# Masked attention with residual on one core: the last batch's outputs, gathers and partial outputs are placed elsewhere, and its short chunk is computed in four blocks

## The chip, the cores and the metric

The kernel runs on one core of a Trainium2 chip. The core has five engines that follow programs of their own and meet through semaphores: PE (matmul, with its weight loads PEld), DVE (VectorE), ACT (ScalarE), POOL (GpSimd) and SP (SyncE). SP does no arithmetic here; it issues DMAs. POOL and ACT issue some too. Sixteen DMA engines carry all of them. The metric is the time of one execution on the device in microseconds; the time before is the median of three runs, 651.81 us (649.6 to 653.38).

## The reference

`x` is 8 x 512 x 1024 (batch, features, tokens), the mask `cond_2048` is 8 x 1024 of zeros and ones, and `Wq`, `Wo` are 512 x 512. All of it is float32.

```python
xt = jnp.transpose(x, (0, 2, 1))
q = xt @ Wq.T                                    # queries, keys and values alike
qh = q.reshape(B, T, NH, dk).transpose(0, 2, 1, 3)       # 8 heads of 64
scores = scale * jnp.einsum('bhqd,bhkd->bhqk', qh, qh)
logits = (scores * cmask + (1.0 - cmask) * NEG) * rmask  # mask on keys, and on queries
attn = jax.nn.softmax(logits, axis=-1)
ctx = jnp.einsum('bhqk,bhkd->bhqd', attn, qh)
out = ctx.transpose(0, 2, 1, 3).reshape(B, T, D) @ Wo.T
return x + jnp.transpose(out, (0, 2, 1))
```

About half of the tokens are masked. A masked token is no key, and as a query all of its logits are zero, so its context is the plain mean of all values.

## The kernel before

The kernel computes attention for the kept tokens of a batch only, at most 543 of them (`NK` = 544), with the mean of all tokens as the last column. The 544 tokens are four chunks of 128 and a short one of 32 (`LAST` = 4, `END` = 32). Two other versions of the program, for masks that keep more tokens, stand behind a branch and do not run.

A batch has four pairs of heads. `pairs` lists all 32 pairs (batch, pair), and the main loop of `late` runs over them; each has five slots, k = 0 to 4, one for each chunk of keys, the short one first. A slot issues `scores` for its chunk (matmuls, then the exponentials on ACT), some fixed steps, and the steps that `slots_of` put into it. The order in the source is the order on each engine: nothing is reordered afterwards, and an engine that waits holds up all that stands behind it. The words (7,1) mean pair 1 of batch 7, the last batch.

The steps that matter here:

- `end_attend`, `go_on_attend`, `attend`, `attend_last`: products of the exponentials with the values (line 730 and 748). `inverses` (824 to 832) makes the reciprocal sums `ris` on DVE. For most pairs `invert` sends them through DRAM (`row<-rt`, `rb<-row`, on SP) to spread them over the partitions; for the last two pairs PE does it in `spread` (810). `contexts` (859 to 868) multiplies the context by them on DVE and gives `cT`. `contexts` of a pair comes two pairs later, at k = 0; for (7,2) it came one pair later, at k = 1 of (7,3).
- `output(b, i)`: chunk i of a batch's output, four matmuls (883), a copy on ACT (892) and a store to `od` in DRAM by POOL (894). For the short chunk `output` already computes four blocks of 128 columns side by side in the four column groups of PE. Batch 6's outputs stand in (7,1) and (7,2).
- `load_rows(b, i)` (941, SP): block i, of eight, of the original tokens from `xd`, into `g`. `fetch(b, i)` (977, POOL): a gather from `od` by the tokens' places, which adds to `g`; a `keep_step` (974) before it ties it to its slot. It waits for all stores of `od`. `finish_blocks(b, i)` (947, DVE): turns `g` into `xr`; after the eighth, SP issues four writes of 512 KB to `out` (954). There is one `xr` buffer. The dictionaries `ROWS_LAST`, `FETCH_LAST` and `FINISH_LAST` say in which slots of batch 7 batch 6's blocks take these steps.
- The last batch ends otherwise: `begin_output` (903, copy 911) makes the product of the first three pairs of each chunk in (7,3), and after `attend_last` `end_output` adds the fourth (919 on PE, 927 on DVE) and stores with SP (933). Then `fetch_last` gathers (963, POOL), `finish_tokens` turns on PE (992), adds on DVE (993) and writes from ACT's queue (994).

`woT` holds its columns in another order, (a, d, f) instead of (d, a, f), which is why `end_output` adds through rearranged views.

Of the kernel before, what the change touches and what calls it, by code (L numbers as in the profile page):

```python
# [13 lines left out]
ALU = mybir.AluOpType  # L14
# [292 lines left out]
def attention_of_kept_tokens(ctx, tc, x, mask, wq, wo, out, ident, wqT, woT, verdict, flag):  # L307


    nc = tc.nc  # L310
    B, D, T = x.shape
    P = 128
    DK = D // NH
    SCALE = 1.0 / math.sqrt(DK)
    ND = D // P
# [4 lines left out]
    A = P // Q  # L320
    NQ = 4
    NC = -(-LONG // P)
    LAST = NC - 1
# [4 lines left out]
    sizes, places = [], []  # L328
# [48 lines left out]
    xs, xbars, xmeans, xds, xins, xcs, parts, searches = {}, {}, {}, {}, {}, {}, {}, {}  # L377
# [292 lines left out]
    es, rbs, cTs, shares = {}, {}, {}, {}  # L670
# [132 lines left out]
    def spread(pair, inv):  # L803

        rb = rbs[pair] = sb.tile([P, W], F32, tag="rb", name="rb_%d_%d" % pair)
        for at, n in ((0, LAST), (LAST, 1)):
            pt = bank("rb_%d_%d" % (pair[1], at))
            for i in range(n):
                for h in range(2):
                    nc.tensor.matmul(  # L810
                        pt[h * DK : (h + 1) * DK, i * P : (i + 1) * P],
                        inv[:, h, at + i : at + i + 1].to_broadcast([P, DK]),
                        ident,
                        start=True,
                        stop=True,
                    )
            nc.scalar.copy(rb[:, at * P : (at + n) * P], pt[:, : n * P])
# [46 lines left out]
    def contexts(pair):  # L864
        sum_last(pair)
        cT, rb = cTs[pair], rbs.pop(pair)
        nc.vector.tensor_tensor(cT, cT, rb[:, :NK], ALU.mult)
        nc.vector.tensor_copy(cT[:, NK - 1 : NK], qTs.pop(pair)[:, W - 1 : W])


    ods, gs, xrs = {}, {}, {}
# [23 lines left out]

    partials = {}

    def begin_output(b, i):

        n = sizes[i]  # L900
        po = bank(f"pa_{b}_{i}")
        for pr in range(ND - 1):
            nc.tensor.matmul(
                po[:n, :],
                cTs[b, pr][:, i * P : i * P + n],
                woT[:, pr, :],
                start=(pr == 0),
                stop=(pr == ND - 2),
            )
        pa = sb.tile([P, D], F32, tag="xin", name=f"pa_{b}_{i}", bufs=NC)  # L910
        nc.scalar.copy(pa[:n, :], po[:n, :])
        partials[i] = pa

    def end_output(b, i):
        n = sizes[i]
        if i == 0:
            ods[b] = dr.tile([NK, D], F32, tag="od", name=f"od_{b}")
        po = bank(f"po_{b}_{i}")
        nc.tensor.matmul(
            po[:n, :],  # L920
            cTs[b, ND - 1][:, i * P : i * P + n],
            woT[:, ND - 1, :],
            start=True,
            stop=True,
        )
        oc = sb.tile([P, D], F32, tag="oc", name=f"oc_{b}_{i}", bufs=NC)
        nc.vector.tensor_tensor(
            oc[:n, :].rearrange("p (d a f) -> p a d f", d=ND, a=A),
            po[:n, :].rearrange("p (a d f) -> p a d f", d=ND, a=A),
            partials[i][:n, :].rearrange("p (a d f) -> p a d f", d=ND, a=A),  # L930
            ALU.add,
        )
        nc.sync.dma_start(ods[b][places[i], :], oc[:n, :])

    def in_blocks(t):
        return t.rearrange("(k f) (a n) -> a f k n", f=Q, a=A)
# [67 lines left out]
    pairs = [(b, pr) for b in range(B) for pr in range(ND)]  # L1004

    def slots_of(p):

        b, pr = pairs[p]
        todo = [[] for _ in range(NC)]
        before = pairs[p - 1] if 0 < p < len(pairs) - 1 else None  # L1010
        behind = pairs[p + 1] if p + 1 < len(pairs) else None
        ahead = pairs[p + 2] if p + 2 < len(pairs) else None

        def do(k, f, *args):
            todo[k].append(lambda: f(*args))

        late = p == 2
        new = pr == 2 and b + 1 < B
        by_vector = nc.vector.tensor_copy

        def project_with_values():
            project(ahead, 0, lambda end: turn_values(behind, end))
            copy_values(behind)

        def mean_with_values():
            pt = bank(f"mean_{b + 1}")
            turn_values(behind, pt[:, KH : KH + P])
            put_mean(b + 1, pt, lambda: copy_values(behind))

        def project_with_top(hf, tag="t"):  # L1030
            project(ahead, hf, lambda to: turn_top(behind, to), tag)
            bias_of(behind)

        if before:
            do(0, go_on_attend, before)
        due = []
        if pr == 1 and b + 1 == B:
            due = [0, 1]
        elif pr > 0 and 0 < b < B - 1:
            due = {1: (0, 1, LAST), 2: (2,), 3: (3,)}[pr]  # L1040
        if not new:
            for i in due:
                do(3, output, b - 1, i)
        if p == 0:
            do(0, project, behind, 1)
            do(1, values, behind)
            do(1, lengths_of, behind)
            do(1, project, ahead, 0)
            do(2, project, ahead, 1)
            do(3, bias_of, behind)  # L1050
        elif late:
            do(1, values, behind)
            do(2, lengths_of, behind)
            do(2, end_attend, before)
            do(2, put_mean, b + 1)
            do(2, collect, b + 1, 0)
            do(3, bias_of, behind)
            do(3, collect, b + 1, 1, by_vector, "a")
            do(3, collect, b + 1, 2, None, "a")
            do(4, collect, b + 1, 3)  # L1060
            do(4, collect, b + 1, 4)
            for hf in range(2):
                do(4, project, ahead, hf, None, "a")
        elif new:
            do(1, mean_with_values)
            do(2, end_attend, before)
            do(3, collect, b + 1, 0, by_vector)
            do(3, collect, b + 1, 1, by_vector)
            do(3, collect, b + 1, 2, by_vector, "a")
            do(3, collect, b + 1, 3, None, "a")  # L1070
            do(3, collect, b + 1, 4, by_vector)
            do(3, lengths_of, behind)
            for i in due:
                do(3, output, b - 1, i)
            do(3, project_with_top, 0)
            do(3, project, ahead, 1, None, "a")
        elif ahead:
            do(1, project_with_values)
            do(2, lengths_of, behind)
            do(2, end_attend, before)  # L1080
            do(3, project_with_top, 1)
        elif behind:
            do(1, output, b - 1, LAST - 1)
            do(1, values, behind)
            do(2, lengths_of, behind)
            do(2, end_attend, before)
            do(3, bias_of, behind)
            do(3, output, b - 1, LAST)
        if p == ND - 1:
            for d in range(ND):  # L1090
                do(3 + d // 2, turn_weights, woT, "wo", d, None, "at"[d // 2], True)
        if pr == 1 and b + 1 == B:
            do(4, output, b - 1, 2)
        if p + 1 == len(pairs):
            for i in range(NC):
                do((1, 1, 2, 3, 4)[i], begin_output, b, i)
        return todo

    def load_weights(w, nm, queue=None):
# [163 lines left out]
    def late(n):  # L1263
# [36 lines left out]
            (1, 1): (6, 7),  # L1300
        }
        FINISH = {(0, 4): (0, 1), (1, 1): (2, 3), (1, 2): (4, 5), (1, 4): (6, 7)}
        FETCH_LAST = {(2, 4): (0, 1, 2), (3, 0): (3, 4, 5), (3, 1): (6, 7)}
        FINISH_LAST = {(3, 1): (0, 1, 2), (3, 2): (3, 4, 5), (3, 3): (6, 7)}
        ROWS = {(2, 2): (0, 1), (2, 3): (2, 3), (3, 0): (4, 5), (3, 2): (6, 7)}
        ROWS_LAST = {(2, 0): (0, 1, 2), (2, 1): (3, 4, 5), (2, 2): (6, 7)}
        for p, pair in enumerate(pairs):
            b, pr = pair
            before = pairs[p - 1] if p else None
            todo = slots_of(p)  # L1310
            for k, c in enumerate(order):
# [5 lines left out]
                if k == 0 and before:  # L1317
                    if p + 1 < len(pairs):
                        invert(before)
                    else:  # L1320
                        inv = inverses(before)
                if p + 1 == len(pairs):
                    if k == 1:
                        spread(before, inv)
                        contexts(before)
                if b > 1:
                    for i in FETCH.get((pr, k), ()):
                        keep_step(pair, c)
# [1 line left out]
                if b + 1 == B:  # L1330
                    for i in FETCH_LAST.get((pr, k), ()):
                        keep_step(pair, c)
# [31 lines left out]
                if b > 0:  # L1364
                    for i in (ROWS if b + 1 < B else ROWS_LAST).get((pr, k), ()):
                        load_rows(b - 1, i)
# [7 lines left out]
                if b + 1 == B:  # L1374
                    for i in FINISH_LAST.get((pr, k), ()):
                        finish_blocks(b - 1, i)
# [134 lines left out]
```

## Time and profile before

| what | us |
|---|---|
| median of three runs | 651.81 |
| the profiled execution | 656.09 |
| its span | 654.4 |
| PE busy in the span | 614.3 |
| ACT, DVE, POOL busy | 378.3, 359.8, 211.1 |
| from the last products on PE (625.64) to the first gather of batch 7 (632.96) | 7.3 |
| from that gather to the end of the span | 21.4 |

A row of the timeline reads: start, length, engine, line, operation, what is written and read, how many instructions are merged in it, and in brackets how long the engine had been idle and what ended that. SPq and ACTq are DMA issues; their length is the issue, not the transfer. A row of a stretch reads: stretch, its length, busy time of PE, PEld, DVE, ACT and POOL with instruction counts, PE's granted clock, the busy share of the DMA engines and GB/s. In the DMA view q1 is SP's queue, q0 POOL's and q10 ACT's; a line of 40 digits is the busy share of the DMA engines in tenths over the window cut in 40.

### The profile page before, as it was taken

Reading aid. Unit: us, or ns where it says so; the run is one execution under the profiler, and the core shown is the slowest. Engines: PE = TensorE matmul, PEld = TensorE weight load, DVE = VectorE, ACT = ScalarE, POOL = GpSimd, SP = SyncE. Lnnn points to the kernel's source line nnn. Section 1 sums busy time; section 2 is a strip of 40 time slices with the busy share of each in tenths; the row PEclk is TensorE's granted clock in tenths of the full one; section 3 lists DMA queues with packets and bytes.
Section 4 is the critical chain, followed back from the end, with each engine's and each line's share of the span. In section 5 each row is a group of like instructions: output and inputs, shape, how many; then the busy total and the mean of one; then the engine's idle time right before and its main releaser. Section 6 shows DMA issues by size and latency. Waiting matters only on the chain. (4 is left out here: it accounts for less than half of the span.)

```text
span 654.4 us, 15913 instructions
## 1 busy us (share of the span) xinstructions
PE 614.3 (94%) x6078; PEld 380.5 (58%) x6078; DVE 359.8 (55%) x1034; ACT 378.3 (58%) x1004; POOL 211.1 (32%) x313
## 2 busy tenths in 40 slices
PE   4789799999999999999999999999999999998964
PEld 3756466656665666566665666566665666554323
DVE  6449556335465566746465558566575425444543
ACT  4266558754766577754776577664775556554400
POOL 5620400140067004830176004720275006305422
PEclk7799899999999999999999999999999999999985
DMA  7666612454588757977598756975795635566677
GB/s 237 187 199 166 233 57 67 141 168 133 147 178 214 244 172 186 180 246 230 172 182 257 228 173 155 199 244 187 196 179 164 198 102 94 111 162 188 112 220 219
DMA packets 94543, 116.62 MB, mean 178 GB/s; under 512 B 11911, under 2 KB 61639, under 8 KB 94462
## 3 DMA queue, kind: packets, MB, share of 16 engines
q1 hardware_dynamic: 74030, 75.20, 38.6%
q0 software_dynamic: 16208, 38.25, 25.2%
q10 hardware_dynamic: 4224, 2.10, 1.1%
q8 instruction: 49, 0.80, 0.5%
q14 instruction: 32, 0.26, 0.1%
HBM read 72.81 MB, written 42.70 MB: 177 GB/s over the span
## 5 line engine op out<-in xcount | busy, mean ns | idle before, releaser
L692 ACT ACTIVATE e<-s,bias 128x544 f32<-128x544 f32 x256 | 180.5, 710 | 75.6 <-PE s L684 58.9
L684 PE MATMUL s<-qT 64*64 64x272 f32 x2048 | 154.8, 398 | 6.5 <-ACT e L692 4.9
L748 PE MATMUL av<-e,v 64*64 64x272 f32 x1920 | 132.4, 392 | 0.0
L598 PE MATMUL pq<-xc,wqT 128*128 128x272 f32 x512 | 131.4, 401 | 0.0
L598 PEld LDWEIGHTS pq<-xc,wqT 128*128 128x128 f32 x512 | 93.3, 190 | 36.8 <-issue 21.0
L684 PEld LDWEIGHTS s<-qT 64*64 64x64 f32 x2048 | 77.2, 133 | 55.8 <-ACT e L692 13.4
L883 PE MATMUL po<-woT,cT 128*128 128x512 f32 (+1 forms) x448 | 108.9, 439 | 0.0
L894 POOL DMA_DIRECT2D od<-oc x56 | 30.2, 544 | 238.5 <-ACT oc L892 237.7
L977 POOL DMA_INDIRECT g<-od,block_origin x56 | 90.1, 1610 | 30.9 <-DVE ends L721 8.1
L748 PEld LDWEIGHTS av<-e,v 64*64 64x64 f32 x1920 | 76.6, 134 | 38.1 <-issue 2.1
L664 DVE TENSOR_REDUCE m<-pq 128x1 f32<-128x128 f32 x28 | 8.2, 292 | 132.0 <-ACT qT L610 107.5
L883 PEld LDWEIGHTS po<-woT,cT 128*128 128x128 f32 (+1 forms) x448 | 46.5, 149 | 54.6 <-issue 53.2
L608 ACT COPY qT<-pq 128x272 f32<-128x272 f32 x64 | 24.6, 385 | 69.7 <-PE pq L655 29.0
L947 DVE STREAM_TRANSPOSE xr<-g 128x512 f32<-128x512 f32 x56 | 57.9, 1099 | 7.6 <-DMA g<-od,block_origin 7.5
L645 DVE TENSOR_REDUCE len<-sq 128x10 f32<-128x640 f32 x32 | 25.8, 805 | 60.4 <-ACT sq L643 60.3
L974 POOL COPY step<-e 1x1 f32<-1x1 f32 x75 | 23.7, 316 | 90.7 <-ACT e L692 90.5
L692 ACT ACTIVATION_READ_ACCUMULATOR e<-s,bias 128x1 f32 x256 | 50.5, 197 | 0.0
L544 POOL DMA_INDIRECT xin<-xd,source x40 | 38.7, 968 | 16.6 <-issue 5.6
L892 ACT COPY oc<-po 128x512 f32<-128x512 f32 (+1 forms) x35 | 18.0, 515 | 44.0 <-PE po L883 43.5
L474 DVE STREAM_TRANSPOSE xt<-x 128x1024 f32<-128x1024 f32 x28 | 34.7, 1241 | 1.5 <-DMA xd<-xt 0.9
L532 DVE TENSOR_SCALAR_CACHE_REDUCE junk<-rank,key 128x1024 f32<-128x1024 f32 (+4 forms) x35 | 34.9, 998 | 0.0
L721 DVE CUSTOM_DVE_ANT_0 junk<-el,part 128x272 f32<-128x272 f32 x64 | 27.3, 427 | 6.6 <-ACT el L709 4.4
(175 smaller groups left out, 674.0 us busy)
## 6 DMA issues: line engine op xcount, KB each, us to landing
xd<-xt SPq DMA_DIRECT2D x120, 128.0 KB
x<-in_x_dram SPq DMA_DIRECT2D x56, 256.0 KB
g<-xd SPq DMA_DIRECT2D x56, 256.0 KB
out_dram<-xr SPq DMA_DIRECT2D x28, 512.0 KB
rb<-row SPq DMA_DIRECT2D x60, 160.0 KB
od<-oc POOLq DMA_DIRECT2D x28, 256.0 KB
rank<-ranks SPq DMA_DIRECT2D x6, 512.0 KB
x<-in_x_dram POOLq DMA_DIRECT2D x8, 256.0 KB
```

What stands on the lines that cost most here:

```text
L474: nc.vector.transpose(xt.rearrange("p k (d f) -> p k d f", d=ND), xs[b][r][:, :, at : at + n].rearrange("p d (k t) -> p k d t", t=Q),)
L532: nc.vector.tensor_scalar(junk[:, :n], rank[:, i * P :], key[:, col], 0.0, ALU.is_le, ALU.add, accum_out=found[:, col])
L544: nc.gpsimd.indirect_dma_start(out=xin[:n, :], out_offset=None, in_=xds[b], in_offset=bass.IndirectOffsetOnAxis(ap=searches[b][2][:n, i : ...
L598: nc.tensor.matmul(pq[:, :KH], wqT[:, d, pr * P : (pr + 1) * P], xcs[b][:, d, cols], start=(d == 0), stop=(d == ND - 1),)
L684: nc.tensor.matmul(ss[h][r * DK : (r + 1) * DK, hf, :KH], qT[heads[h], c * P + r * DK : c * P + (r + 1) * DK], qT[heads[h], queries[hf]], ...
L692: nc.scalar.activation(e[:, :, h, :], ss[h][:, :, :KH], AF.Exp, bias=bias, scale=SCALE, accum_out=sums[pair[1] % 2][:, h, c : c + 1],)
L721: nc.vector.tensor_tensor_reduce(junk[:, :KH], e[:, 0, h, :], parts[b], 1.0, 0.0, ALU.mult, ALU.add, ends[pr % 2][:, h : h + 1])
L748: nc.tensor.matmul(avs[pair][hf][head, :KH], v[keys, c, head], e[keys, hf, h, :], start=(c == 0 and not crossed), stop=(c == LAST - 1 and ...
L883: nc.tensor.matmul(po[k * n : (k + 1) * n, :w], cTs[b, pr][:, i * P : i * P + n], woT[:, pr, k * w : (k + 1) * w], start=(pr == 0), stop=( ...
L894: nc.gpsimd.dma_start(ods[b][places[i], k * w : (k + 1) * w], oc[k * n : (k + 1) * n, :w])
L947: nc.vector.transpose(xr.rearrange("p (d a) (t i) -> p a d t i", a=A, i=NT)[..., i], gs[b, i].rearrange("p (a d f) -> p a d f", a=A, f=Q),)
L977: nc.gpsimd.indirect_dma_start(out=gs[b, i], out_offset=None, in_=ods[b], in_offset=bass.IndirectOffsetOnAxis(ap=block_origin[:, b, i : i ...
```

## The change

Four things are changed, all for batches 6 and 7, and nothing else.

1. Batch 6's outputs all stand in (7,1): chunk 0 in slot 2, 1 and 2 in slot 3, 3 and the short one in slot 4. Before, (7,1) had 0 and 1 in slot 3 and 2 in slot 4, and (7,2) had 3 in slot 1 and the short one in slot 3.
2. Batch 6's blocks: loads in (7,1) slots 2 to 4 and (7,2) slot 0, gathers in (7,2), turning from (7,2) slot 3 to (7,3) slot 2. Before, loads in (7,2), gathers from (7,2) slot 4 to (7,3) slot 1, turning in (7,3) slots 1 to 3.
3. In (7,3) `spread` and `contexts` of (7,2) stand in slot 0 and not in slot 1, and the partial outputs in slots 1, 2, 3, 4, 4 and not in 1, 1, 2, 3, 4.
4. The short chunk of batch 7 is computed in four blocks of 128 columns side by side, in `begin_output` as in `end_output`, each with a strided view of `woT`; its addition runs over 128 x 128 and not 32 x 512, and it is stored with four DMAs, two from SP's queue and two from ACT's.

```diff
+    def add_product(b, i, pr, po, start, stop):
+        n = sizes[i]
+        parts = P // n
+        w = D // parts
+        tokens = cTs[b, pr][:, i * P : i * P + n]
+        if parts == 1:
+            nc.tensor.matmul(po, tokens, woT[:, pr, :], start=start, stop=stop)
+            return
+        in_order = woT[:, pr, :].rearrange("p (a d f) -> p d a f", a=A, d=ND)
+        for k in range(parts):
+            nc.tensor.matmul(
+                po[k * n : (k + 1) * n, :w],
+                tokens,
+                in_order[:, k * ND // parts : (k + 1) * ND // parts, :, :],
+                start=start,
+                stop=stop,
+            )
...
         for pr in range(ND - 1):
-            nc.tensor.matmul(po[:n, :], cTs[b, pr][:, i * P : i * P + n], woT[:, pr, :], ...
+            add_product(b, i, pr, po, pr == 0, pr == ND - 2)
-        nc.scalar.copy(pa[:n, :], po[:n, :])
+        nc.scalar.copy(pa[:, :w], po[:, :w])
...
-        nc.sync.dma_start(ods[b][places[i], :], oc[:n, :])
+        else:
+            nc.vector.tensor_tensor(oc[:, :w], po[:, :w], partials[i][:, :w], ALU.add)
+        for k in range(parts):
+            queue = nc.scalar if k % 2 else nc.sync
+            queue.dma_start(ods[b][places[i], k * w : (k + 1) * w], oc[k * n : (k + 1) * n, :w])
...
         if pr == 1 and b + 1 == B:
-            due = [0, 1]
+            due = [1, 2]
+            do(2, output, b - 1, 0)
...
-            do(1, output, b - 1, LAST - 1)
             do(1, values, behind)
...
-            do(3, output, b - 1, LAST)
...
         if pr == 1 and b + 1 == B:
-            do(4, output, b - 1, 2)
+            do(4, output, b - 1, LAST - 1)
+            do(4, output, b - 1, LAST)
         if p + 1 == len(pairs):
             for i in range(NC):
-                do((1, 1, 2, 3, 4)[i], begin_output, b, i)
+                do((1, 2, 3, 4, 4)[i], begin_output, b, i)
...
-        FETCH_LAST = {(2, 4): (0, 1, 2), (3, 0): (3, 4, 5), (3, 1): (6, 7)}
-        FINISH_LAST = {(3, 1): (0, 1, 2), (3, 2): (3, 4, 5), (3, 3): (6, 7)}
+        FETCH_LAST = {(2, 0): (0,), (2, 1): (1, 2), (2, 2): (3, 4), (2, 3): (5, 6), (2, 4): (7,)}
+        FINISH_LAST = {(2, 3): (0,), (2, 4): (1, 2), (3, 1): (3, 4, 5), (3, 2): (6, 7)}
-        ROWS_LAST = {(2, 0): (0, 1, 2), (2, 1): (3, 4, 5), (2, 2): (6, 7)}
+        ROWS_LAST = {(1, 2): (0, 1), (1, 3): (2, 3), (1, 4): (4, 5), (2, 0): (6, 7)}
...
-                if p + 1 == len(pairs):
-                    if k == 1:
-                        spread(before, inv)
-                        contexts(before)
+                if p + 1 == len(pairs) and k == 0:
+                    spread(before, inv)
+                    contexts(before)
```

More of the change, by code (lines that the diff above doesn't have):

```diff
@@ L896, in attention_of_kept_tokens @@
     partials = {}
+    def add_product(b, i, pr, po, start, stop):
[15 more added lines that the diff above has]
+            )
     def begin_output(b, i):
-        n = sizes[i]
         po = bank(f"pa_{b}_{i}")
         for pr in range(ND - 1):
[L903 to L909, printed above, removed]
+            add_product(b, i, pr, po, pr == 0, pr == ND - 2)
+        w = D // (P // sizes[i])
         pa = sb.tile([P, D], F32, tag="xin", name=f"pa_{b}_{i}", bufs=NC)
-        nc.scalar.copy(pa[:n, :], po[:n, :])
+        nc.scalar.copy(pa[:, :w], po[:, :w])
         partials[i] = pa
@@ L915, in end_output @@
         n = sizes[i]
+        parts = P // n
+        w = D // parts
         if i == 0:
@@ L918, in end_output @@
         po = bank(f"po_{b}_{i}")
[L919 to L925, printed above, removed]
-        oc = sb.tile([P, D], F32, tag="oc", name=f"oc_{b}_{i}", bufs=NC)
[L927 to L933, printed above, removed]
+        add_product(b, i, ND - 1, po, True, True)
+        oc = sb.tile([P, D], F32, tag="oc", name=f"oc_{b}_{i}", bufs=NC)
+        if parts == 1:
+            nc.vector.tensor_tensor(
+                oc.rearrange("p (d a f) -> p a d f", d=ND, a=A),
+                po.rearrange("p (a d f) -> p a d f", d=ND, a=A),
+                partials[i].rearrange("p (a d f) -> p a d f", d=ND, a=A),
+                ALU.add,
+            )
+        else:
[3 more added lines that the diff above has]
+            queue.dma_start(ods[b][places[i], k * w : (k + 1) * w], oc[k * n : (k + 1) * n, :w])
     def in_blocks(t):
```

## The prediction

> **What bounds the kernel now.** I read, in this order: the page's busy times, the busy times by stretch of the last batch, the chain of waits, the timeline of the last 100 us engine by engine, and the DMA view in windows where a transfer is late.
>
> ```profile
> span 654.4 us, 15913 instructions
> PE 614.3 (94%) x6078; PEld 380.5 (58%) x6078; DVE 359.8 (55%) x1034; ACT 378.3 (58%) x1004; POOL 211.1 (32%) x313
> ```
> ```profile
> 552.40:576.40 24.00, 24.00 (x195) 13.42 (x198) 14.79 (x38) 11.94 (x31) 8.31 (x11) 1.00 0.51 104
> 576.40:595.50 19.10, 18.32 (x214) 10.13 (x206) 6.54 (x27) 9.98 (x26) 3.23 (x7) 1.00 0.77 221
> 595.50:617.80 22.30, 20.54 (x128) 8.44 (x126) 10.64 (x17) 10.24 (x25) 13.31 (x15) 1.00 0.69 123
> ```
> ```profile
> 640.55 5.73 DMA g<-od,origin
> ```
> The three stretches are the pairs (7,1), (7,2) and (7,3); the first two columns are the length and PE's busy time. PE sets the pace, so moving matmuls is free unless PE comes to wait. After PE's last attention, the chain is stores, gathers and writes; its longest piece is one gather of 5.73 us. So the change is worth the PE waits that it ends or makes, plus the distance from PE's last products to the first gather of batch 7.
>
> **The PE side, in the trace of before.**
>
> ```profile
> 561.69 7.13 PE L883 MATMUL po<-woT,cT 128*128 128x512 f32 x16
> ...
> 571.78 3.70 PE L883 MATMUL po<-woT,cT 128*128 128x512 f32 x8
> ...
> 588.59 1.08 PE L883 MATMUL po<-woT,cT 128*32 128x128 f32 x32
> ...
> 597.49 1.13 PE L684 MATMUL s<-qT 64*64 64x272 f32 x12 [0.81 <-ACT el L709]
> 598.56 1.31 PE L810 MATMUL rb<-ident,ris 128*64 128x128 f32 x20
> ...
> 602.74 3.70 PE L903 MATMUL pa<-woT,cT 128*128 128x512 f32 x8 [0.95 <-DVE cT L867]
> ...
> 615.14 2.76 PE L903 MATMUL pa<-woT,cT 128*32 128x512 f32 x6
> ...
> 620.28 1.31 PE L810 MATMUL rb<-ident,ris 128*64 128x128 f32 x20 [1.31 <-DVE ris L831]
> ...
> 625.64 4.87 PE L919 MATMUL po<-woT,cT 128*128 128x512 f32 x10
> ```
> A matmul of 512 columns leaves two records; one output of four matmuls costs 7.13 / 2 = 3.57 us, the short one in blocks 1.08.
>
> **Moved outputs: 0 by themselves.** Pair (7,1) gets one full output (3.57) and the short one (1.08), 4.65 us; (7,2) loses the same. Output 0 now stands in slot 2, so all of (7,1) behind it is 3.57 us later. What covers ACT in (7,2) is gone: its exponentials of 128x544 come in pairs,
>
> ```profile
> L692 ACT ACTIVATE e<-s,bias 128x544 f32<-128x544 f32 x256 | 180.5, 710 | 75.6 <-PE s L684 58.9
> ...
> L692 ACT ACTIVATION_READ_ACCUMULATOR e<-s,bias 128x1 f32 x256 | 50.5, 197 | 0.0
> ```
> each 0.71 + 0.20, so 1.8 a pair, and PE's fillers left in slots 1 to 3 are mostly shorter. I estimate 0.5 us for each of three slots, 1.5. It counts 0, because PE waits longer behind it (below); without that wait it costs 1.5.
>
> **Short chunk in blocks: -1.95.** The partial goes from 2.76 us to 12 matmuls, 24 records of the kind that takes 1.08 for 32: 0.81. This one reads its moving columns as four runs of 32 where the row reads one run of 128. If that undid the gain, it would be 0, if it were free 1.95; I take 1.95, the nearest row by shape. The last product of the chunk shrinks likewise; that helps only through the first gather, below.
>
> **The wait on ris at 620.28: -1.31.** DVE comes late there because it still turns gathered blocks; the new order turns the last ones in slot 2. Cover if this is wrong: none, the 1.31 stays.
>
> **Gathers and their turning: the term that decides.** DVE works in order, and before the inverses that PE's `spread` needs at the start of (7,3) it must now turn blocks 0, 1 and 2, so wait for three gathers. When do these land?
>
> ```profile
> 569.75 0.58 POOL L894 DMA_DIRECT2D od<-oc  x1 [2.82 <-ACT oc L892]
> ...
> 571.36 0.29 DVE L664 TENSOR_REDUCE m<-pq 128x1 f32<-128x128 f32 x1 [7.20 <-ACT qT L610]
> ...
> 574.07 5.36 SPq L954 DMA_DIRECT2D out_dram<-xr  x4
> ...
> 576.39 0.54 POOL L894 DMA_DIRECT2D od<-oc  x1 [6.06 <-ACT oc L892]
> ...
> 590.29 1.99 POOL L894 DMA_DIRECT2D od<-oc  x4 [5.90 <-ACT oc L892]
> ...
> 591.43 0.23 DVE L859 TENSOR_TENSOR rb<-rb 128x64 f32<-128x64 f32 x1 [1.99 <-DMA rb<-row]
> ...
> 594.72 0.18 DVE L832 TENSOR_SCALAR ris<-ends,pads 128x2 f32<-128x2 f32 x1
> ...
> 598.27 1.70 POOL L977 DMA_INDIRECT g<-od,block_origin  x1 [5.82 <-DVE ends L721]
> ...
> 603.37 1.11 DVE L947 STREAM_TRANSPOSE xr<-g 128x512 f32<-128x512 f32 x1 [0.50 <-DMA g<-od,block_origin]
> ...
> 607.98 1.10 DVE L947 STREAM_TRANSPOSE xr<-g 128x512 f32<-128x512 f32 x1 [1.14 <-DMA g<-od,block_origin]
> ```
> ```profile
> DMA packets 1080, 1.07 MB, mean 215 GB/s; under 512 B 32, under 2 KB 1080, under 8 KB 1080
> q1 hardware_dynamic: 1080, 1.07, 92.4%
> ```
> ```profile
> DMA  9999889979999999998877889996410000000000
> ```
> ```profile
> DMA  0000000000000000000997997200000000000000
> q0 software_dynamic: 80, 0.26, 16.1%
> ```
> The DMA fences are the windows 576:581, 581:588 and 569:573 (40 digits each, tenths). In the second window SP's writes of batch 5 are drained at 581 + 30 x 0.175 = 586.25. In the first, POOL's store issued at 576.39 moves nothing: all 1080 packets are SP's. In the third, with no other traffic, a store of 256 KB issued at 569.75 is over at 571.6, 1.9 us later.
>
> Step by step: (1) DVE's maximum at 571.36, which waits for PE behind the outputs, is 3.57 us later, and so are the last two turnings of batch 5 and SP's writes behind them: 577.6, drained at 589.8. (2) The short output ends on PE at 575.48 + 3.57 + 1.08 = 580.1 (575.48 is where the third output of before ends, as 571.78 + 3.70 in the timeline); POOL issues its four stores from 580.7 to 582.7, into those writes. (3) The first gather needs them landed. Lower bound: clean, 582.2 + 1.9 and then 1 us to start, 585. By the stores at 590.29, whose gather came 8.0 us after the first issue: 588.7. If they wait until the writes are drained: 589.8 and a start, 590.6. I take 590.6, because the store at 576.39 met the same writes. (4) The third turning began 9.7 us after the first gather (598.27 to 607.98): 600.3, and ends at 601.4. (5) From the contexts of the pair before to the inverses took 591.43 to 594.90, 3.5 us: ris at 604.9. (6) PE would be at `spread` at about 597.5 (595.5, the 1.5 of ACT, the scores before it), so it stands still for some 7 us. Then 1.31 for spread, 1.1 for the scores of block 0, 1.8 for two matmuls: the third matmul of partial 0 runs at 609.1, where before it ran at 602.74: +6.4. The old waits of 0.81 and 0.95 are inside that. `rb<-row` of (7,1) is later by 3.57 as well, 591.43 becomes 595.0; DVE asks for it at 601.4, so 0 (3.57 if no gather held DVE). The loads of blocks 0 to 5, moved on SP's queue ahead of batch 5's writes, run beside batch 5's last gathers, which DVE turns only at 575.6: 0. Blocks 6 and 7 load behind `rb<-row`, before their gathers' turn: 0.
>
> **The clock after such a wait: +1.7.**
>
> ```profile
> 72.74 2.32 PE L684 MATMUL s<-qT 64*64 64x272 f32 x14 [4.22 <-ACT e L692]
> ```
> ```profile
> 73.30:76.70 3.40, 3.38 (x34) 1.82 (x36) 0.00 (x0) 2.67 (x8) 1.86 (x2) 0.50 0.24 77
> ```
> After 4.22 us without work PE's granted clock was 0.50 for 3.4 us: half of that, 1.7, is lost. A wait of 7 us should bring at least as much; 0 if it is cut under 4 us, 3.4 for twice the stretch. I take 1.7.
>
> **The end: -1.8.**
>
> ```profile
> 619.32 5.28 SPq L954 DMA_DIRECT2D out_dram<-xr  x4
> ...
> 627.52 4.07 SPq L933 DMA_DIRECT2D od<-oc  x5
> ...
> 632.96 1.00 POOL L963 DMA_INDIRECT g<-od,origin  x1 [19.56 <-DMA od<-oc]
> ```
> Now the first gather starts 7.3 us after the last products begin (625.64 to 632.96), because the stores go out behind 2 MB of batch 6's writes on SP's queue. With the last turning at some 616 + 1.7 those writes, which take 12 us like the ones at 574.07, are drained before the new stores at about 631. A clean store of 1.9 to 2.5 us, issued 1.9 after the products and up to 2.9 for the blocks, gives 5.5: a gain of 1.8 (0 if the writes slip late enough to meet them, 2.3 at best). The short chunk's four DMAs stand two on SP's queue and two on ACT's, with nothing else waiting behind them but the later stores, 0.3 us each.
>
> **Sum** against the profiled execution, 656.09 (span 654.4, 1.7 around it): +6.4 + 1.7 - 1.95 - 1.31 - 1.8 = +3.0, so 659.1, a ratio of 1.0046. The profiled execution lies 0.65% above the median of the three, 651.81; on that the forecast is 654.8. A difference of 0.5% (3.3 us) is about what a measurement of this kernel can tell from none, so the forecast stands at the upper edge of "the same".
>
> **Rivals.** *The stores are not held by the writes (faster).* The short chunk's stores land in 2 us, the first gather starts at 585.0 instead of 590.6, ris is ready at 599.3, PE waits under 2 us and the clock stays: 3.0 - 5.6 - 1.7 = -4.3, time 647.5. It turns to a gain when the first gather starts before about 588. For it: the stores at 590.29 were through in 8 us beside 2 MB of loads. Against it: the empty window 576:581. The Trainium skill's page "DMA: Bandwidth & Descriptors", section "Queues, rings and completion order", says that a DMA engine takes turns between its queues packet by packet; by that rule the stores would pass beside the writes and this rival would hold. The window with 1080 packets of one queue and none of the other does not agree with it.
>
> *The gathers are slower (slower).* They start where `rb<-row` and the last two block loads run: by the sizes below, two of each are 0.83 MB, at the 215 GB/s of window 576:581 3.9 us of DMA.
>
> ```profile
> g<-xd SPq DMA_DIRECT2D x56, 256.0 KB
> ...
> rb<-row SPq DMA_DIRECT2D x60, 160.0 KB
> ```
>  If all of it goes ahead of gather 2, ris comes 4 us later: +7.0, time 658.8. For it: each gather of before waited for its data although nothing else ran (0.50 and 1.14 us at DVE). Against: the loads were issued earlier than the data phase of gather 0.
>
> *The blocks do nothing.* The partial in blocks still takes 2.76: +1.95, so +5.0, time 656.8. Against it the 1.08 row.
>
> **Chances.** The forecast's case 0.56, half of it above the 0.5% line or nearly (its size moves by 1 us with each us of the first gather; 588.7 gives +1.1, 592 gives +4.4; alone 652.5 to 657); stores free 0.18; gathers slower 0.19; blocks void 0.07. Faster 0.18, within 0.5% 0.36, slower 0.46. The range takes the free stores at its low end and the slow gathers at its high end: 647.5 to 658.8.
>
> **What will show it.** PE's row of `spread` in (7,3) with an idle time of some 7 us released by DVE ris; a stretch of granted clock 0.50 there; DVE's turnings 0 to 2 waiting for gathers just before it; the writes of batch 5 at 577.6; the partial of the short chunk at 0.8; no idle time before the second `spread`; the first gather of batch 7 5.5 us after the last products. A `spread` without idle time makes the forecast wrong on the fast side. If the first gather starts after 592, it is wrong on the slow side.

## The result, and the profile after

The changed kernel takes 657.29 us (median, 654.06 to 660.34) where the kernel before, measured beside it, takes 652.50 (649.44 to 655.42): a ratio of 1.0076, with a 95% interval of 1.0054 to 1.0099. It is slower by 4.8 us (3.5 to 6.5). A ratio with its interval, here and below, is estimated from the runs of the two kernels; it is near the quotient of the two medians and not equal to it.

The first lines of the changed kernel's page:

```profile
span 655.1 us, 15977 instructions
PE 614.9 (94%) x6102; PEld 382.3 (58%) x6102; DVE 358.4 (55%) x1034; ACT 378.4 (58%) x1004; POOL 211.1 (32%) x313
```
This span is only 0.7 us above that of before, 654.4, because the two executions began differently. Two stretches, first of before, then of the changed kernel:

```profile
8.50:25.60 17.10, 5.46 (x26) 5.46 (x27) 11.64 (x25) 6.54 (x13) 9.05 (x13) 0.50 0.83 261
```
```profile
3.60:20.70 17.10, 7.41 (x31) 6.12 (x31) 12.43 (x29) 5.63 (x13) 7.14 (x16) 1.00 0.92 283
```
PE had half its clock for 17 us at the start of the one and not in the other, where both kernels do the same. So I count from an event that stands ahead of all that is changed, the start of the projection in slot 1 of (7,1), first before and then changed:

```profile
555.29 2.10 PE L598 MATMUL pq<-xc,wqT 128*128 128x272 f32 x8
```
```profile
550.37 2.10 PE L598 MATMUL pq<-xc,wqT 128*128 128x272 f32 x8
```
From there the changed kernel is 4.92 us ahead; a time of its trace plus 4.92 stands on the prediction's scale. "At +34.7" below means 34.7 us after this projection.

The pairs (7,1), (7,2) and (7,3) of the changed kernel, and the one stretch at half clock in them:

```profile
547.50:576.30 28.80, 28.80 (x234) 15.51 (x238) 15.65 (x43) 12.91 (x33) 9.71 (x13) 1.00 0.62 157
576.30:591.60 15.30, 14.76 (x174) 7.85 (x166) 2.87 (x11) 9.04 (x24) 7.67 (x12) 1.00 0.77 185
591.60:619.70 28.10, 20.47 (x146) 9.66 (x144) 14.51 (x36) 10.30 (x25) 7.14 (x9) 0.88 0.66 135
597.70:604.40 6.70, 4.02 (x36) 2.80 (x36) 3.48 (x13) 0.76 (x2) 1.83 (x3) 0.50 0.71 115
```
(7,1) is longer and (7,2) shorter by the two outputs. (7,3) has 28.10 - 20.47 = 7.6 us in which PE does nothing; before it had 1.8. The timeline of the changed kernel, PE and the engines behind it together:

```profile
570.24 0.29 DVE L664 TENSOR_REDUCE m<-pq 128x1 f32<-128x128 f32 x1 [8.25 <-ACT qT L610]
...
572.95 5.37 SPq L968 DMA_DIRECT2D out_dram<-xr  x4
...
575.26 0.54 POOL L894 DMA_DIRECT2D od<-oc  x1 [6.11 <-ACT oc L892]
575.98 1.99 POOL L894 DMA_DIRECT2D od<-oc  x4 [0.17 <-issue]
...
585.05 1.70 POOL L991 DMA_INDIRECT g<-od,block_origin  x1 [6.86 <-DMA out_dram<-xr]
...
591.55 1.11 DVE L961 STREAM_TRANSPOSE xr<-g 128x512 f32<-128x512 f32 x1 [5.38 <-DMA rb<-row]
...
594.75 1.09 DVE L961 STREAM_TRANSPOSE xr<-g 128x512 f32<-128x512 f32 x1 [2.09 <-DMA g<-od,block_origin]
...
596.04 1.09 DVE L961 STREAM_TRANSPOSE xr<-g 128x512 f32<-128x512 f32 x1 [0.19 <-DMA g<-od,block_origin]
...
596.98 0.20 DVE L859 TENSOR_TENSOR rb<-rb 128x64 f32<-128x64 f32 x1
...
600.24 0.18 DVE L832 TENSOR_SCALAR ris<-ends,pads 128x2 f32<-128x2 f32 x1
...
600.38 2.40 PE L810 MATMUL rb<-ident,ris 128*64 128x128 f32 x20 [7.63 <-DVE ris L831]
...
604.63 2.84 PE L905 MATMUL pa<-woT,cT 128*128 128x512 f32 x6
...
618.96 0.86 PE L909 MATMUL pa<-woT,cT 128*32 128x128 f32 x24
...
620.72 1.26 PE L810 MATMUL rb<-ident,ris 128*64 128x128 f32 x20
...
626.02 1.13 PE L905 MATMUL po<-woT,cT 128*128 128x512 f32 x2
...
631.61 1.00 POOL L977 DMA_INDIRECT g<-od,origin  x1 [31.82 <-DVE worst L1414]
```
Read it from the wait backwards. PE stands still for 7.63 us until DVE has `ris` (600.42). DVE made it right after the contexts (596.98), and these right after three turnings, each of which waited for data; the first, at 591.55, had waited 5.38 (the row names `rb<-row`, which a turning does not read; it needs gather 0, issued at 585.05). Gather 0 waited for the short chunk's stores, issued at 575.98 (its row names `out_dram<-xr`, which a gather does not read either; in f4, the same kernel, it names `len`). What held those is in the DMA view of the changed kernel, window 573:581, then two lines of window 581:585; a queue's line gives packets, MB and busy share, and the last number of an issue's line is the median time from issue to landing:

```profile
DMA  0000698989898989998989898989899899899998
q1 hardware_dynamic: 1486, 1.48, 80.9%
q0 software_dynamic: 9, 0.04, 1.2%
od<-oc POOLq DMA_DIRECT2D x1, 256.0 KB, 8.1
od<-oc POOLq DMA_DIRECT2D x4, 16.0 KB, 7.2
```
```profile
q1 hardware_dynamic: 706, 0.62, 57.8%
q0 software_dynamic: 199, 0.29, 21.5%
```
Up to 581 SP's queue moves 1486 packets, of batch 5's writes nearly all, and POOL's moves 9, none of them in the first 5.1 us after the first store's issue. From 581 on the two queues move side by side, 706 packets and 199, and nearly all traffic is over at 584.6. The stores take 8.1 and 7.2 us to land. In f4 POOL's packets begin some 1.5 us sooner (115 in the same window, counted from the projection), the stores land after 6.5 and 6.9 us, and gather 0 comes 0.4 us sooner.

The account from the projection on, all kernels in one table (us; "first" and "second" are the two `spread` in (7,3), with PE's idle time ahead of them; "to the end" runs from the first gather of batch 7 to the end of the span):

| kernel | projection at | gather 0 | first: start, idle | partials end | second: idle | last products | first gather of batch 7 | to the end |
|---|---|---|---|---|---|---|---|---|
| before | 555.29 | +42.99 | +43.27, 0 | +62.62 | 1.31 | +70.35 | +77.67 | 21.40 |
| changed | 550.37 | +34.68 | +50.01, 7.63 | +69.45 | 0 | +75.65 | +81.24 | 23.51 |
| f4, changed once more | 551.04 | +34.28 | +49.84, 7.46 | +69.30 | 0 | +75.50 | +81.10 | 21.18 |
| e1, turned late | 552.17 | +34.03 | +45.59, 3.21 | +64.68 | 0 | +70.89 | +76.51 | 21.28 |
| e2, PE kept busy | 553.18 | +33.95 | +50.33, 1.74 | +67.83 | 0 | +74.03 | +79.64 | 21.67 |
| e3, no writes | 554.87 | +30.80 | +45.33, 2.76 | +65.57 | 0 | +71.77 | +77.20 | 22.68 |
| e4, writes later | 554.94 | +31.15 | +42.83, 0 | +60.34 | 3.10 | +71.14 | +77.08 | 22.32 |
| f1, writes split | 550.74 | +33.20 | +42.31, 0 | +59.89 | 0 | +66.09 | +72.27 | 22.76 |
| g2, f1 once more | 554.90 | +33.18 | +44.55, 0 | +62.27 | 0 | +68.47 | +74.03 | 21.15 |
| f2, blocks alone | 551.30 | +42.85 | +43.27, 0 | +60.72 | 2.92 | +71.37 | +77.49 | 21.10 |
| f3, blocks and spread | 553.42 | +42.73 | +41.31, 0 | +58.82 | 4.62 | +71.49 | +77.12 | 22.21 |
| g1, changed, no blocks | 552.99 | +34.10 | +50.02, 7.63 | +71.77 | 0 | +77.98 | +83.21 | 21.98 |

The first gather of batch 7 comes 3.6 us later than before. What follows it takes 21.1 to 23.5 us in these profiles, 23.51 and 21.18 for the very same kernel, so no part of it is put down to the change.

### The profile page after: what moved, and what is told of

The parts are those of the page before. It is cut to its first block, busy times and chain, and to the rows that moved or that the text cites. A ratio compares the mean times of both kernels' runs of the same rounds, so it can differ in the third digit from the quotient of the medians.

```text
span 655.1 us, 15977 instructions
## 1 busy us (share of the span) xinstructions
PE 614.9 (94%) x6102; PEld 382.3 (58%) x6102; DVE 358.4 (55%) x1034; ACT 378.4 (58%) x1004; POOL 211.1 (32%) x313
## 5 line engine op out<-in xcount | busy, mean ns | idle before, releaser
L988 POOL COPY step<-e 1x1 f32<-1x1 f32 x77 | 25.2, 327 | 83.5 <-ACT e L692 83.4
L474 DVE STREAM_TRANSPOSE xt<-x 128x1024 f32<-128x1024 f32 x28 | 34.7, 1241 | 1.4 <-DMA xd<-xt 0.9
L493 ACT ACTIVATE junka<-x 128x512 f32<-128x512 f32 x48 | 30.2, 628 | 1.1
```

Of the source, the lines that this page charges most:

```text
L474: nc.vector.transpose(xt.rearrange("p k (d f) -> p k d f", d=ND), xs[b][r][:, :, at : at + n].rearrange("p d (k t) -> p k d t", t=Q),)
L493: nc.scalar.activation(junk, xs[b][r][:, d, :], AF.Copy, accum_out=xbars[b][:, d, r : r + 1])
```

## The experiments

**The turnings put back (e1).** All of the change stays but the slots in which DVE turns batch 6's blocks.

```diff
-FINISH_LAST = {(2, 3): (0,), (2, 4): (1, 2), (3, 1): (3, 4, 5), (3, 2): (6, 7)}
+FINISH_LAST = {(3, 1): (0, 1, 2), (3, 2): (3, 4, 5), (3, 3): (6, 7)}
```

> The changed kernel, but batch 6's blocks are turned in (7,3) slots 1 to 3, as before; the gathers stay early. Theory (DVE's turnings of blocks 0 to 2 hold the inverses, so PE): the contexts of (7,1) start when rb lands, about 592.5 in the changed kernel's trace and not 597.0, so ris is ready some 4.6 us sooner, PE's wait at the first spread falls from 7.6 to about 3 us, and the time falls by 4.6 us or, if the clock is not halved then, 6.5: 651 to 653. Rival (the wait belongs to the sums or the gathers' traffic, not to DVE's order): the wait stays at 7 us, the time at 657.

Measured: 653.56 against 654.99 of before, ratio 0.9982 (0.9957 to 1.0008). Its timeline, and the stretch behind the wait:

```profile
594.34 0.23 DVE L859 TENSOR_TENSOR rb<-rb 128x64 f32<-128x64 f32 x1 [6.49 <-DMA rb<-row]
...
597.76 1.43 PE L810 MATMUL rb<-ident,ris 128*64 128x128 f32 x20 [3.21 <-DVE ris L831]
```
```profile
598.80:602.20 3.40, 3.40 (x24) 1.37 (x21) 2.34 (x7) 1.71 (x5) 1.88 (x3) 0.50 1.01 169
```
PE's wait falls from 7.63 to 3.21 us, as expected, and the last products come 4.8 us earlier. So the order on DVE makes the larger part of the wait. The rest is a second wait that stood behind it: DVE has nothing to do for 6.49 us until `rb<-row` of (7,1) has landed. SP issued that load at 588.06 (+35.9), behind batch 5's writes and the `row` stores on its queue.

**PE kept busy (e2).** Seven matmuls on no one's behalf ahead of the first `spread`.

```diff
                 if p + 1 == len(pairs) and k == 0:
+                    hold = bank("hold")
+                    for _ in range(7):
+                        nc.tensor.matmul(hold, ident, woT[:, 0, :], start=True, stop=True)
                     spread(before, inv)
```

> The changed kernel with seven matmuls of 128x512 whose result nobody reads, some 6.2 us of work, in PE's queue ahead of the first spread in (7,3). Theory (the wait costs a halved clock besides): the granted clock stays 1.0, spread and the scores after it take 1.3 and 1.1 us and not 2.4 and 2.0, the third matmul of partial 0 is 1.5 to 2 us sooner, time 655.3. Rival (PE then waits for DVE's contexts anyway): no more than 0.5 us, 657.

Measured: 657.46 against 654.99, ratio 1.0053 (1.0023 to 1.0083).

```profile
595.50 6.28 PE L1339 MATMUL hold<-woT,ident 128*128 128x512 f32 x14
...
603.51 1.31 PE L810 MATMUL rb<-ident,ris 128*64 128x128 f32 x20 [1.74 <-DVE ris L832]
```
```profile
595.40:609.40 14.00, 12.26 (x74) 5.68 (x72) 8.82 (x26) 3.79 (x10) 5.73 (x7) 1.00 0.72 138
```
`ris` is as late as in the changed kernel (the first `spread` at +50.33 and not +50.01), but the clock stays at 1.00, `spread` takes 1.31 and not 2.40, and the partials end at +67.83 and not +69.45: the clock's share is 1.6 us, 1.9 counted from each kernel's own `spread`, as the theory had it. The traces show this and not the times: the interval of the ratio overlaps that of the changed kernel, 1.0054 to 1.0099.

**Batch 5's four writes left out (e3).** This kernel leaves out the result of batch 5.

```diff
+                if (b, pr, k) == (B - 1, 1, 4):
+                    rests.clear()
                 while rests:
```

> The changed kernel without the four writes of batch 5's result from SP's queue in (7,1), 2 MB left out. Theory (the short chunk's stores to od stand behind these writes): the stores land 2 us after their issue and not 6.6 to 7.5, the first gather starts at about 580.5 and not 585.05, rb lands at about 580, the third turning ends about 592, ris is ready at 595 or sooner, PE waits 2 us or less, the clock stays; with 1.9 for the clock some 7.5 us less, 649.8. Rival (the gathers are slow by themselves, or POOL's queue is): the first gather starts within 1 us of 585, time 656 to 657.

Measured: 653.46 against 654.99, ratio 0.9985 (0.9962 to 1.0008). POOL's five stores are issued from 579.8 to 582.0. The DMA view, window 579.5:585, then the timeline:

```profile
DMA  0000000000999940311400310140100000000000
q0 software_dynamic: 208, 0.33, 16.3%
```
```profile
585.67 1.70 POOL L991 DMA_INDIRECT g<-od,block_origin  x1 [2.98 <-DMA row<-rt]
...
595.80 1.11 DVE L961 STREAM_TRANSPOSE xr<-g 128x512 f32<-128x512 f32 x1 [0.99 <-DMA g<-od,block_origin]
...
600.19 2.40 PE L810 MATMUL rb<-ident,ris 128*64 128x128 f32 x20 [2.76 <-DVE ris L831]
```
The stores begin to move at 579.5 + 10 x 0.1375 = 580.9, and the last of the small ones are through by 583.5; gather 0 comes at +30.80, 3.9 us earlier. So batch 5's writes do hold the stores; the prediction's rival had put 5.6 us on it. But the expectation, a wait of 2 us or less with the clock whole, was missed: with the stores free PE still waits 2.76 us, with half its clock behind it. Three turnings still stand ahead of the inverses, and the third began at 595.80, ten us after gather 0 was issued.

**The four writes one slot later, with the turnings put back (e4).**

```diff
-                while rests:
+                while rests and (b, pr, k) != (B - 1, 1, 4):
```

> The kernel with late turning (first run of this study), and the four writes of batch 5's result issued one slot later, at the end of (7,2) slot 0, behind row, rb and the last two block loads on SP's queue. Theory: rb of (7,1) lands near 581 and holds nobody, the inverses wait for the sums alone, PE's wait at the first spread is under 0.5 us, no halved clock; against the changed kernel 7.6 + 1.9 less, 647.8, 0.7% faster than the kernel before. Rival (the writes then collide with the gathers, and the turning and the second spread come late): a wait of 1 us or more at the second spread, time 650 to 653.

Measured: 653.79 against 654.99, ratio 0.9974 (0.9954 to 0.9995).

```profile
610.74 7.62 DVE L961 STREAM_TRANSPOSE xr<-g 128x512 f32<-128x512 f32 x8 [7.95 <-DMA out_dram<-xr]
...
619.45 2.40 PE L810 MATMUL rb<-ident,ris 128*64 128x128 f32 x20 [3.10 <-DVE ris L832]
```
The first wait is gone. Now the one `xr` buffer is read by the late writes, DVE's turnings wait 7.95 us for it, and the second `spread` pays 3.10 us, at half clock again. The gain at the first place is given back at the second, as the rival had it.

**Two writes at the old place, two a slot later (f1, and again g2).** The turnings put back as in e1, and:

```diff
                 while rests:
+                    if (b, pr, k) == (B - 1, 1, 4) and len(rests) <= A // 2:
+                        break
                     rests.popleft()()
```

> The kernel with late turning (e1_turn_late), and of the four writes of batch 5's result two stand where they are in the changed kernel and two after row, rb and the last two block loads, at the end of (7,2) slot 0. Theory (PE's first wait is rb behind the writes, its second wait comes when the writes drain after the turnings could begin): both waits are gone, PE's products of the last batch begin 66.5 us after the projection in (7,1) slot 1, against 70.35 in the kernel before and 75.65 in the changed one, the first gather of batch 7 at 72; 5 us less than the kernel before, ratio 0.992. Rival (rb still stands behind two writes): a wait of 1 us or more at the first spread, ratio 0.996 or above.

> The kernel with split writes and late turning once more: ratio 0.993 again, between 0.990 and 0.996, products of the last batch 66 us after the projection in (7,1) slot 1. If its gain came from the tail's scatter, which runs from 21.1 to 23.5 us, the products would be there later or the ratio above 0.996.

Measured: 647.50 against 651.59, ratio 0.9933 (0.9907 to 0.9959), and in the second measurement 650.31 against 655.01, ratio 0.9919 (0.9888 to 0.9950). This version beats both kernels. SP issues `rb<-row` at +32.7 here, 3.2 us sooner than in e1, and DVE has it at +37.7 and not +42.2. Of f1:

```profile
span 645.8 us, 15977 instructions
```
```profile
588.39 0.22 DVE L859 TENSOR_TENSOR rb<-rb 128x64 f32<-128x64 f32 x1 [2.03 <-DMA rb<-row]
...
593.05 1.31 PE L810 MATMUL rb<-ident,ris 128*64 128x128 f32 x20
...
601.64 7.62 DVE L961 STREAM_TRANSPOSE xr<-g 128x512 f32<-128x512 f32 x8 [3.50 <-DMA out_dram<-xr]
...
611.53 1.26 PE L810 MATMUL rb<-ident,ris 128*64 128x128 f32 x20
```
```profile
585.00:625.00 40.00, 36.10 (x276) 16.73 (x274) 21.18 (x59) 14.50 (x37) 13.54 (x17) 1.00 0.78 182
```
Neither `spread` waits and the clock stays whole. Against before, the last products come 4.26 us earlier: the first `spread` starts 0.96 earlier and the blocks save 1.90 (the partials end 2.73 earlier, so 0.13 is lost between), the second wait is gone, 1.31, and 0.22 lies around the second `spread`. In g2 the first `spread` starts at +44.55, 2.2 us later than in f1, and the last products at +68.47, where 66 was expected, without idle time ahead of the `spread`: there PE had half its clock for 3.4 us inside (7,2), which f1 shows nowhere. The stretch of g2:

```profile
592.20:595.60 3.40, 3.40 (x16) 1.60 (x16) 2.60 (x11) 1.12 (x4) 2.97 (x4) 0.50 1.06 280
```
What set that off was not tried.

f1 shows a second thing, beside f3 below. In neither does the first `spread` wait, and in both it stands in slot 0; but batch 6's outputs are moved in f1 and not in f3, and it starts at +42.31 in the one and +41.31 in the other (+42.83 in e4, moved too). So the moved outputs cost some 1.0 to 1.5 us when no wait hides them, near the 1.5 that the prediction estimated for that case.

**The blocks alone, put into the kernel before (f2).** `add_product` and the new `begin_output` and `end_output`, nothing else.

> The kernel before with the short chunk of batch 7 in four blocks and nothing else. Theory (the second spread waits for inverses that stand behind the last turned blocks, whatever PE saves ahead of it): the partial takes 0.86 and not 2.76 us, the wait at the second spread grows from 1.3 to 3.2, the first gather of batch 7 comes at the same time within 0.5 us; ratio 0.998 to 1.001. Rival (the saving stands by itself, as the sum in the prediction has it): 1.95 less, ratio 0.997, no longer wait.

**The blocks, and `spread` and the partials moved (f3).** As f2, with the third part of the change:

```diff
-                if p + 1 == len(pairs):
-                    if k == 1:
-                        spread(before, inv)
-                        contexts(before)
+                if p + 1 == len(pairs) and k == 0:
+                    spread(before, inv)
+                    contexts(before)
...
-                do((1, 1, 2, 3, 4)[i], begin_output, b, i)
+                do((1, 2, 3, 4, 4)[i], begin_output, b, i)
```

> The kernel before with the blocks, and with spread and contexts of (7,2) in slot 0 and the partial outputs in slots 1, 2, 3, 4, 4 as in the changed kernel; outputs, gathers and turnings of batch 6 as before. Theory: PE saves the waits of 0.81 and 0.95 besides the 1.9 and loses all of it at the second spread, where the wait is 4.5 to 5 us; so long a wait halves the clock for 3.4 us; ratio 1.000 to 1.003. Rival: the savings add up, 3.7 us, ratio 0.994.

Measured: f2 651.29 against 651.59, ratio 0.9979 (0.9952 to 1.0005); f3 654.01, ratio 1.0026 (1.0004 to 1.0047). The second `spread`, first of f2, then of f3:

```profile
616.01 2.40 PE L810 MATMUL rb<-ident,ris 128*64 128x128 f32 x20 [2.92 <-DVE ris L831]
```
```profile
617.94 2.40 PE L810 MATMUL rb<-ident,ris 128*64 128x128 f32 x20 [4.62 <-DVE ris L832]
```
The partials end 1.9 us earlier in f2 and 3.8 in f3, and the second `spread` starts at +64.71 and +64.52, where it started at +64.99 before. The interval of f2's ratio holds its theory and its rival alike; the wait decides between them. What PE saves it waits for, because DVE turns gathered blocks ahead of the second `ris`, and the longer wait halves the clock. The last products come 1.0 and 1.1 us later than before. So the parts of the change on PE bring nothing unless the turnings end earlier too: that is what its second part is needed for.

**The changed kernel with the old short chunk (g1), and as it is (f4).** g1 has the old `begin_output` and `end_output`, all else changed.

> The changed kernel with the short chunk of batch 7 as before, 32 x 512 in one matmul each; all else changed. In the changed kernel the second spread does not wait, so there the saving of the blocks should be whole: the partial takes 2.8 and not 0.86 us, the second spread comes 1.9 us later, the first gather about 2 us later, ratio to the kernel before some 0.003 above the changed kernel's 1.006 to 1.008, 1.009 to 1.011. Rival (the saving is lost in the chain of stores and gathers behind): the ratio stays at 1.006 to 1.008.

> The changed kernel as it is. Beside the runs of this call it gives its ratio on this chip, 1.0076 expected, and a second look at the stretch from the first gather of batch 7 to the end, 23.5 us in the changed kernel's first profile and 21.4 in that of before. If 23.5 belongs to the change it comes again; if it is a scatter between executions it lies between 21.3 and 22.7 as in the four runs before.

Measured: g1 660.57 against 655.01, ratio 1.0087 (1.0057 to 1.0118); f4 655.41 against 651.59, ratio 1.0059 (1.0038 to 1.0080). In g1 the partials of chunk 3 and the short chunk are one group:

```profile
619.23 5.54 PE L903 MATMUL pa<-woT,cT 128*128 128x512 f32 x12
```
5.54 less 2.84 for chunk 3 leaves 2.70 for the short one, where the blocks take 0.86. The last products come 2.3 us later than in the changed kernel and 2.5 later than in f4. In the changed order the saving arrives whole at the last products, because nothing waits behind it, and the first gather of batch 7 comes 2.0 us later (+83.21 against +81.24). The ratios of g1 and f4 differ the same way, but their intervals overlap. The 23.5 us from that gather to the end did not come again in f4, which had 21.2.

## Why the prediction was right

It forecast +0.46%, at the edge of what can be told from none, from a new wait of PE; measured was +0.76% (0.54 to 0.99), with that wait. The direction and the mechanism were right, the size was 0.3% short, and the prediction had given only 0.46 to a loss above its 0.5% line. Step by step, times on the prediction's scale:

- **The writes of batch 5 later by 3.57, at 577.6.** 572.95 + 4.92 = 577.87. Right.
- **The stores held until the writes are drained, gather 0 at 590.6.** 585.05 + 4.92 = 589.97. The time is right, and e3 shows that the writes are the cause by taking them away. The reason is right in part: the stores wait some 4 to 5 us without moving, but then they move beside the rest of the writes and are through about when these are. The trace of before has this too, in the prediction's own second window: from 582 to 583 POOL's queue moves 42 packets and SP's 123, 3 us before the writes are drained. The rival with the free stores falls: they took 7.2 us. By the rule that the prediction cites from the Trainium skill's page "DMA: Bandwidth & Descriptors", section "Queues, rings and completion order", the stores would have passed beside the writes from the start; the window with 1486 packets of SP's queue and 9 of POOL's does not agree with it, the 706 and 199 packets after 581 do.
- **Third turning ends at 601.4, `ris` at 604.9, a wait of some 7.** 596.04 + 1.09 + 4.92 = 602.05, 605.34, and 7.63; PE is at `spread` at 597.67, forecast 597.5. Right within 0.7, in part by luck: gather 0 came 0.6 sooner than forecast, and from it to the third turning it took 11.0 us and not 9.7. The rival of slower gathers falls as it was priced: they were 1.3 slower, not 4.
- **+6.4 for the wait and 1.7 for the clock.** The third matmul of partial 0 cannot be read off the merged row, but the partials end 6.83 us later although the blocks save 1.90: 8.7 together, against 8.1. e2 puts 1.6 to 1.9 of it on the clock. Both terms right, the first short by some 0.6.
- **-1.95 for the blocks.** The short chunk's partial takes 0.86 us, forecast 0.81; 2.76 - 0.86 = 1.90. The rival "blocks do nothing" falls, by g1 too.
- **-1.31, the second wait.** No idle time ahead of the second `spread`. Right, and f2 and f3, which keep the old turnings, have a wait there.
- **-1.8 at the end.** 631.61 - 626.02 = 5.59 from the last products to the gather, where before had 7.3 and the forecast 5.5: -1.7. Right; g1, without the blocks, has 5.2, so the blocks are not what brings it.

The sum of what was measured: 8.7 - 1.9 - 1.3 - 0.2 (between the partials and the second `spread`) = +5.3 at the last products, as the table has it, and +3.6 at the first gather, forecast +3.0. The term that was too small is the wait. The 3.6 stands inside the measured 3.5 to 6.5, at its low end, and the second measurement of the same kernel gives +3.8 (655.41 against 651.59). What of the 4.8 goes beyond 3.6 the traces do not tell, since the part behind the first gather scatters by 2 us.

Three points the prediction had wrong or did not have, besides the writes and stores that move side by side. It had `rb<-row` land at 595.0; e1 shows 594.34 - 552.17 + 555.29 = 597.5, so without the turnings PE would still have waited 3.2 us. Its price of nothing for that wait stands, because the turnings hide it; for the case without them it had put 3.57. It charged the halved clock only to waits of over 4 us, and e1, e3, e4 and f2 show it at waits of 2.76 to 3.21. And it treated the stores as the one thing that decides ("turns to a gain when the first gather starts before about 588"): in e3 gather 0 comes at 555.29 + 30.80 = 586.1, and the ratio is 0.9985 with an interval that holds 1. The wait in DVE's order remains, shorter.

## What to carry to other kernels

An engine that works in order must not be given work that waits for a DMA ahead of work that the bounding engine needs: here three early turnings on DVE cost PE 4.4 of 7.6 us of waiting, and with them behind the inverses the change can no longer be told from none (0.9957 to 1.0008). A saving that stands ahead of a fixed event is swallowed (f2, f3: 1.9 and 3.8 us saved, nothing gained at the last products), so look first for what the next wait is released by. Large writes placed just ahead of small stores and loads on the critical path delay these by several us (gather 0 came 3.9 us sooner without them); splitting them around the small transfers, with the turnings late, turned a loss of 0.8% into a gain of 0.7% to 0.8%.

## What the runs showed of the hardware

- **With waits of 2.8 to 3.2 us PE's clock fell to half** (e1, e3, e4, f2), for 3.4 us or, in e3, for 6.8:

```profile
599.20:606.00 6.80, 5.81 (x38) 3.64 (x39) 3.62 (x15) 2.10 (x6) 1.21 (x1) 0.50 0.66 94
```
  In e3 the half clock begins at 599.2, 1.8 us into a wait that ends at 600.19; in e1 it begins at 598.8, 1.0 us after the wait is over. Waits of 1.74 us (e2) and 1.31 us (before) left the clock whole. The Trainium skill's page "TensorE: Matmul & The Clock Gate", section "HAM oscillation — how this bites in real kernels", gives the rule "no PE-idle gaps >~3.4µs". These shorter waits do not keep to it. Filling most of the 7.63 us with seven matmuls (e2) does keep the clock. That a wait alone sets off the half clock is not shown: in g2 it came when PE had not waited longer than 0.63 us at a time just before.
- **Stores on POOL's queue, issued into 2 MB of writes of SP's queue, do not move for some 4 to 5 us, and then move beside them**: 9 packets against 1486, then 199 against 706; 6.5 to 8.1 us to land. Without the writes the first packets move 1.1 us after the first issue (580.9, 579.8), and all are through by 583.5, 1.5 us after the last. What holds them at first is not shown.
- **A gather of one block takes some 6 us even without the writes**: in e3 the third turning waits for data until 595.80, and gather 2 was issued at 589.56, 6.2 us before; the gathers and the last loads share the DMA engines there.
- **Narrow blocks are cheap even with a strided moving operand**: the short chunk in 24 records of 128 columns, read as runs of 32, took 0.86 us, against 2.70 to 2.76 in one row of 512.
